# Held products at named places, a reordered first convolution and joins in small lots in a four-image, four-layer convolution kernel

## The chip, the cores and the metric

The kernel runs on one core of one Trainium2 chip. The metric is the device time of one execution in microseconds (us), as a median of three runs.

## The reference

Four layers work on x of shape (4, 256, 64, 64), all in fp32. Each adds to x what it computes from a group-normalised x (`_gn`: 32 groups, so 8 channels each):

```
x = x + L0(_gn(x))   # 3x3 convolution 256->256, group norm, relu = xs; then attention over 4096
                     #   pixels: softmax(theta^T phi) g, 128 wide; 1x1 to 256, group norm,
                     #   times 0.1, plus xs
x = x + L1(_gn(x))   # channel norm; q, k, v of 4 heads x 32; softmax of q over the head's channels,
                     #   of k over pixels; context = k v^T; out = context q; 1x1 to 256; channel norm
x = x + L2(_gn(x))   # two small nets (1x1, relu, mean) generate a depthwise 3x3 kernel for each
                     #   channel and a 256x256 pointwise matrix for each image; apply both, plus bias
x = x + L3(_gn(x))   # a router (mean, 64, softmax over 4 experts) mixes four 256x256 matrices;
                     #   apply the mixture
```

## The kernel before, in words

One image is held as two halves of 128 channels (h, or oh for outputs) by 4096 pixels. The four images go through a pipeline written out by hand: every engine's instructions run in the order in which the program emits them (`manual_schedule`). TensorE is given the order by interleaving two generators: `attend(b)`, 256 steps of logits (`pf`), exponentials (`pr`, ScalarE), row sums (`tot`, VectorE) and weighted values (`py`), and a `Chain`, which carries the layers after the attention of the image before (`tail`: `nonlocal_out`, `linear_attention`, `generated`, `mixed`) and then the convolution of the next image (`convolve`). A chain's parts yield costs; each time their sum times the chain's rate passes 1, one attention step is emitted and `tick` runs the functions that were put off with `later(n, f)`. The rate is 1.5 beside image 0's attention, 0.86 beside those of images 1 and 2, 1.24 beside that of image 3.

**Convolution.** The 3x3 convolution is done with transformed filters: six filter rows a (0 to 5) and, inside a row, four products k in the order 1, 2, 0, 3. `down` makes the rows of an input by VectorE, `across` the operand `v` of a product, `products` runs eight matmuls into two PSUM banks (`ps_conv`, L399), `joined` adds them, and `joining` adds a whole filter row into the four output rows y0 to y3: for a = 2 three operations for each half, for a = 4 six. In `convolve` these joins of row 2 are put off by one tick, both halves together; those of row 4 go into a list, `rest`, and leave it three per tick through `some`. `convolve_first` does image 0, where no attention runs beside it: rows 0, 1, 2 and 5 are taken as plain matmuls over shifted rows (`row_products`, `ps_row`, L431), rows 3 and 4 as products; filters for the later images are made by `filter_across` and stored to DRAM (12 DMAs each on SP). Then come statistics (`stats`, L389), the group norm (`group_finish`: aggregate L295, two small matmuls `pm` L300 and `pv` L309 with VectorE steps between and after them, and a root on POOL, L206) and `normed_relu`.

**End phase.** The last layer of image 2 (`mixed`) does not run beside image 3's attention: its 16 products (`product`: four matmul instructions `ps_ex`, L1086, into one bank; then a sum `res` on VectorE, L117, and a store on SP) are put into a list `held`. The last chain, `end`, runs image 3's tail after its attention and takes them out. `w.room` says how many may go; each tick takes one while there is room, and its sum is emitted one tick later.

In that tail, `linear_attention` normalises 512 pixels at a time (`normed`, ScalarE), sums squares (`norms`: `ps_ss`, L752, and a root on POOL), multiplies (`qkv`: `ps_qkv`, L765), and accumulates the context; a small chain (`cm`, `ps_cm`, `ps_w2`) follows, then eight rounds of `outputs` (`ps_o`, L830, four squares on ScalarE, root on POOL), `scaled` and `added` (transposes `ps_zt`, L853). `generated` computes the hidden layer (`ps_h`, L903), normalises into xp, gets the tap factors dk and sets nine diagonal matrices `diag` (ScalarE, L996). Its eight parts (c, h) of 1024 pixels are split for the last image: five (`mine`) are done by VectorE, `centre` on ScalarE (L941) and eight taps (L117, 1.3 us each), three (`others`) by TensorE with the diagonals (`ps_dw`, L984), nine for each 512 pixels, let out by a credit per tap. `pointwise` (`ps_pw`, L949) and its sums follow each pair of parts. `mixed` computes the router and `wm` and runs image 3's own 16 products.

Of the kernel before, what the change touches and what calls it, by code (L numbers as in the profile page):

```python
# [10 lines left out]
ALU = mybir.AluOpType  # L11
# [3 lines left out]
NH = 2  # L15
HW = 64
# [27 lines left out]
class Chain:  # L44
# [3 lines left out]
    def __init__(self, layers, rate=1.0, held=()):  # L48
        self.layers, self.rate, self.due = layers(self), rate, []
        self.held, self.room = held, 0  # L50

    def fill(self):

        if self.room > 0 and self.held:
            self.room -= 1
            self.later(1, self.held.pop(0)())
# [9 lines left out]
    def tick(self):  # L66

        due = [(k - 1, f) for k, f in self.due]
        self.due = [d for d in due if d[0] > 0]
        for k, f in due:  # L70
            if k <= 0:
                f()
        self.fill()
# [13 lines left out]
def conv_preact_fast(ctx: ExitStack, tc: tile.TileContext, guard, x, wc, wtpg, ww, wqkv, wout, w1cat, wd2,  # L87
# [199 lines left out]
    def stats_tile():  # L287
        return sp.tile([P, NH, 8, 6], F32, name="st")
# [203 lines left out]
    def convolve(w, b):  # L492
# [19 lines left out]
        def join(a, k, ps):  # L512
            dst = joined(a, k, ps)
            if k == 3 and a == 4:

                for oh in range(NH):
                    rest.extend(joining(a, oh, dst[oh]))
                for j in range(4):
                    w.later(1 + j, lambda: some(3))
                for j in range(3):  # L520
                    w.later(5 + j, lambda j=j: stats(j))
            elif k == 3:
                some(len(rest))
                for oh in range(NH):
                    w.later(1, lambda oh=oh: rows_joined(a, oh, dst[oh]))
# [25 lines left out]
    def convolve_first(w):  # L551
# [27 lines left out]
        two = row_products(2, ra)  # L579
# [5 lines left out]
        for oh in range(NH):  # L585
            rows_joined(2, oh, two[oh])
        for i, (a, k, v, f) in enumerate(four):
            if i + 1 < TX:
                joined(*three[i + 1])
            four[i] = (a, k, products(a, k, v, f))  # L590
        y3 = row_products(5, rb)
        for a in (0, 1, 2, 5):
            filter_across(a)
        for i in range(1, TX):
            t = joined(*four[i])
        for oh in range(NH):
            rows_joined(4, oh, t[oh])
# [96 lines left out]
    def nonlocal_out(w, b, big, k4, xs_in):  # L694
# [18 lines left out]
        w.room += 2  # L713
# [3 lines left out]
        st = stats_tile()  # L717
        for i, (c, h) in enumerate(PARTS):
            cols = bass.ts(c, CH)
            wy, xs = parts[i]  # L720
            stt(big[:, h, cols], wy, sc[:, h:h + 1], xs, ALU.mult, ALU.add)
            if i + ahead < len(PARTS):
                parts.append(load_parts(i + ahead))
            yield 0.6
            for s in range(2):
                nc.vector.bn_stats(st[:, h, 2 * c + s, :], big[:, h, bass.ts(2 * c + s, 512)])
            yield 0.6
        return st, sh


    def linear_attention(w, b, big, qT, k4, st, sh, alone):
        w.room += 2
# [25 lines left out]
        def qkv(xg, rinv):  # L758
# [3 lines left out]
            for j in range(4):  # L762
                ps = bank("ps_qkv")
                for h in range(NH):
                    nc.tensor.matmul(ps[:, 0:3 * HID], xg[:, h, bass.ts(j, P)], wqkv_s[:, h, :],  # L765
                                     start=(h == 0), stop=(h == NH - 1))
                nc.scalar.activation(qk[:, j, :], ps[:, 0:2 * HID], AF.Exp, scale=rinv[:, j:j + 1])  # L767
                nc.scalar.activation(v1[:, j, 0:P], ps[:, 2 * HID:3 * HID], AF.Copy, scale=rinv[:, j:j + 1])
                yield 0.125
# [20 lines left out]
        ready = ahead[0], norms(ahead[1])  # L790
        last = None
        for c in range(NC):
# [4 lines left out]
            if c + 1 < NC:  # L797
                ready = ahead[0], norms(ahead[1])
# [4 lines left out]
        w.room += 2  # L803
        context(NC - 1, *last)
        rk = sp.tile([P, 1], F32, name="rk")
# [13 lines left out]
        stt(w2, pw[:, 0:NH * P], HD * float(HD) ** -0.5, bo_s, ALU.mult, ALU.add)  # L819
        yield 1  # L820
# [37 lines left out]
        for c in range(NC):  # L858
# [4 lines left out]
            last = scaled(*zb)  # L863
            yield 0.6
        yield 1
        added(NC - 1, last)
        return st
# [4 lines left out]
    def generated(w, b, big, k4, st, sh, diag):  # L872
# [35 lines left out]
        for c in range(N // 512):  # L908
# [4 lines left out]
            if diag is not None and h == 1:  # L913
                nc.vector.tensor_scalar(*normed, rstd[:, h:h + 1], nb[:, h:h + 1], ALU.mult, ALU.add)
            else:
                nc.scalar.activation(*normed, AF.Identity, bias=nb[:, h:h + 1], scale=rstd[:, h:h + 1])
            yield 0.5
# [6 lines left out]
        nc.tensor.matmul(ppl[:, 0:2 * R], ones[0:HT * HP, :], pd, start=True, stop=True)  # L924
        pb = sp.tile([P, 2 * R], F32, name="pb")
# [67 lines left out]
        products, credit = taps_by_products(others), 0.0  # L993
        if diag is not None:
            for k in range(9):
                nc.scalar.activation(diag[:, k, :], ident, AF.Copy, scale=dk[:, 9 + k:10 + k])  # L996
        dw = {mine[0]: centre(mine[0])}
        slices = [load_wp2(0), load_wp2(1)]
        for n, i in enumerate(mine):
            if n + 1 < len(mine):  # L1000
                dw[mine[n + 1]] = centre(mine[n + 1])
            for wait in taps(i):

                credit += 18 * len(others) / (8 * (len(mine) - 1))
# [25 lines left out]
    def mixed(w, b, big, k4, st, sh, held):  # L1030
# [4 lines left out]
        w.room += 7  # L1035
# [23 lines left out]
        nc.vector.tensor_scalar(al, al, asum, None, ALU.mult)  # L1059
        wm = k2("wm")  # L1060
# [32 lines left out]

        for c in range(N // 512):
# [45 lines left out]
    with tc.manual_schedule(engines={E.PE, E.Activation, E.DVE, E.Pool, E.SP}):  # L1140
# [22 lines left out]
        for room, _ in zip((2, 0, 2, 1), attention):  # L1163
            end.room += room
            end.tick()
            if room == 2:
                end.fill()
        run(last)
        while held or end.due:
            end.room += 1  # L1170
            end.tick()
# [584 lines left out]
```

## Time and profile before

| | |
|---|---|
| median of 3 runs | 3176.08 us (3174.74 to 3176.4) |
| the profiled execution | 3175.36 us, span 3173.5 us |
| mean granted TensorE clock | 0.986 |
| busy share: TensorE, VectorE, ScalarE, POOL | 96%, 65%, 36%, 4% |
| first convolution, to the first `ps_tp` | 0 to 152.6 us |
| end phase, from the end of image 3's attention steps | about 2862 to 3173.5 us |

The page divides the span into 40 slices of 79.3 us; each digit is an engine's busy share in tenths. A timeline row holds the start, the duration, the engine, the line, the operation, its output and inputs with shapes, the count, and in brackets the idle time of the engine before it with what released it. fp32 matmuls of a 128x512 operand appear as two records each; four records are one held product.

### The profile page before, as it was taken

The numbers are of one execution on the slowest core, as the hardware profiler recorded it, in microseconds if no ns is written. First come the engines' busy times: TensorE is split into PE (matmuls) and PEld (weight loads), VectorE is DVE, ScalarE is ACT, GpSimd is POOL, SyncE is SP. The second block draws the span as 40 slices with busy tenths as digits, with TensorE's granted clock in tenths as the row PEclk, the third lists the DMA queues.
The fourth block names the chain that finished last, engine by engine and source line by source line (L and its number), as shares of the span: only waits on it lengthen the run. The fifth ranks groups of instructions, "written<-read, shape, count | busy, mean of one in ns | idle before, by whom it ended". The sixth has DMA issues, their size and how long they took to land.

```text
span 3173.5 us, 24226 instructions
## 1 busy us (share of the span) xinstructions
PE 3035.6 (96%) x8526; PEld 1472.2 (46%) x8526; DVE 2075.4 (65%) x2605; ACT 1132.1 (36%) x2099; POOL 129.6 (4%) x175
## 2 busy tenths in 40 slices
PE   6899999999999999999999999999999999996887
PEld 3354444445564444444565444444545544443533
DVE  8636676442547995777536896878363768855575
ACT  2133224333555332313364432312445453333520
POOL 0000000000010000000011000000100100000100
PEclk9999999999999999999999999999999999998999
DMA  5520113001100023113300102310410010121102
GB/s 182 169 45 24 33 35 65 7 14 47 67 11 27 14 73 119 37 37 67 113 10 1 40 20 83 105 41 30 110 64 1 11 34 13 47 73 47 45 6 74
DMA packets 73985, 161.68 MB, mean 51 GB/s; under 512 B 7936, under 2 KB 39424, under 8 KB 70912
## 3 DMA queue, kind: packets, MB, share of 16 engines
q1 hardware_dynamic: 69248, 143.27, 13.3%
q0 software_dynamic: 4608, 16.78, 2.9%
q8 instruction: 70, 1.15, 0.2%
q14 instruction: 59, 0.48, 0.0%
HBM read 103.40 MB, written 73.40 MB: 56 GB/s over the span
## 4 chain that ended last, share of the span: by engine, by line
PE 79%; DVE 13%; issue 5%; ACT 2%; DMA 0%; POOL 0%; SPq 0%; POOLq 0%; ACTq 0%
PE pf L637 23%; PE py L676 23%; PE ps_conv L399 8%; PE ps_qkv L765 5%; DVE dw L117 4%; PE ps_tp L613 4%; PE ps_ex L1086 3%; PE ps_pw L949 3%; DVE tot L114 2%; PE ps_g L618 2%; PE ps_wy L660 2%; PE ps_o L830 1%; PE ps_ctx L785 1%; PE ps_ss L752 1%; PE pss L649 1%
## 5 line engine op out<-in xcount | busy, mean ns | idle before, releaser
L638 ACT ACTIVATE pr<-pf 128x512 f32<-128x512 f32 x1024 | 604.4, 596 | 1229.2 <-PE pf L637 1216.0
L637 PE MATMUL pf<-tpg 128*128 128x512 f32 x2048 | 968.3, 595 | 1.4 <-ACT pr L638 1.4
L676 PE MATMUL py<-pr,tpg 128*128 128x512 f32 x2048 | 962.1, 592 | 3.0 <-ACT pr L638 2.9
L114 DVE TENSOR_TENSOR tot<-tot,pr 128x1024 f32<-128x1024 f32 x448 | 546.2, 1219 | 253.1 <-ACT pr L638 251.5
L676 PEld LDWEIGHTS py<-pr,tpg 128*128 128x128 f32 x2048 | 388.8, 190 | 494.5 <-issue 479.3
L637 PEld LDWEIGHTS pf<-tpg 128*128 128x128 f32 x2048 | 382.3, 190 | 444.4 <-issue 419.8
L117 DVE SCALAR_TENSOR_TENSOR dw<-xp,dk,dw 128x1008 f32<-128x1008 f32 x224 | 282.9, 1267 | 7.0 <-ACT dw L941 3.6
L399 PE MATMUL ps_conv<-v,u 128*128 128x512 f32 x576 | 261.7, 601 | 12.7 <-issue 9.0
L399 PEld LDWEIGHTS ps_conv<-v,u 128*128 128x128 f32 x576 | 110.8, 193 | 154.4 <-issue 147.3
L765 PE MATMUL ps_qkv<-wqkv_s,xg 128*128 128x384 f32 x384 | 130.3, 489 | 0.0
L613 PE MATMUL ps_tp<-big,wtpg_s 128*128 128x512 f32 x256 | 117.1, 601 | 3.0 <-ACT big L488 3.0
L114 DVE TENSOR_TENSOR tpg<-ps_g,bg_s 128x512 f32<-128x512 f32 x32 | 22.1, 691 | 144.7 <-PE ps_g L618 144.7
L206 POOL TENSOR_TENSOR rstd<-rstd,half 128x2 f32<-128x2 f32 x24 | 16.8, 700 | 2445.2 <-DVE rstd L311 2251.5
L949 PE MATMUL ps_pw<-dw,pk 128*128 128x512 f32 x224 | 103.8, 597 | 10.3 <-DVE dw L117 10.3
L651 DVE RECIPROCAL inv<-pss 128x512 f32<-128x512 f32 x32 | 107.3, 3352 | 7.2 <-PE pss L649 7.2
L773 DVE TENSOR_REDUCE qs<-qk 128x16 f32<-128x512 f32 x24 | 16.5, 686 | 123.4 <-ACT qk L767 123.4
L765 PEld LDWEIGHTS ps_qkv<-wqkv_s,xg 128*128 128x128 f32 x384 | 72.0, 190 | 52.4 <-issue 8.6
L114 DVE TENSOR_TENSOR v<-ra 128x1024 f32<-128x1024 f32 x72 | 86.7, 1219 | 0.4
L614 ACT ACTIVATE tpg<-ps_tp,btp_s 128x512 f32<-128x512 f32 x64 | 43.8, 687 | 118.7 <-PE ps_tp L613 118.5
L949 PEld LDWEIGHTS ps_pw<-dw,pk 128*128 128x128 f32 x224 | 42.7, 192 | 65.1 <-issue 51.2
L613 PEld LDWEIGHTS ps_tp<-big,wtpg_s 128*128 128x128 f32 x256 | 47.6, 193 | 54.5 <-issue 50.0
L832 ACT ACTIVATE junk<-ps_o 128x256 f32<-128x256 f32 x128 | 49.2, 384 | 63.6 <-PE ps_o L830 60.6
(278 smaller groups left out, 2887.1 us busy)
## 6 DMA issues: line engine op xcount, KB each, us to landing
u<-filters SPq DMA_DIRECT2D x144, 128.0 KB, 2.3
xp<-in_x_dram SPq DMA_DIRECT2D x16, 1024.0 KB, 6.2
xs_d<-big POOLq DMA_DIRECT2D x32, 512.0 KB, 11.6
wy_d<-wt SPq DMA_DIRECT2D x32, 512.0 KB, 3.0
out_dram<-res SPq DMA_DIRECT2D x64, 256.0 KB, 2.0
wy<-wy_d SPq DMA_DIRECT2D x28, 512.0 KB, 5.3
xs<-xs_d SPq DMA_DIRECT2D x24, 512.0 KB, 5.3
wp<-in_wp_dram SPq DMA_DIRECT2D x16, 512.0 KB, 4.6
```

The costliest lines, as they stand in the source:

```text
L114: nc.vector.tensor_tensor(o, a, b, op)
L117: nc.vector.scalar_tensor_tensor(o, a, s, b, op0, op1)
L399: nc.tensor.matmul(ps[oh], u(oh, h), v[:, bass.ts(h, 512)], start=(h == 0), stop=(h == NH - 1))
L613: nc.tensor.matmul(ps, wtpg_s[:, h, k, :], big[:, h, cols], start=(h == 0), stop=(h == NH - 1))
L618: nc.tensor.matmul(ps[:, j, :], big[:, h, bass.ts(4 * c + j, P)], wtpg_s[:, h, 2, :], start=(h == 0), stop=(h == NH - 1))
L637: nc.tensor.matmul(pf, phi[:, bass.ts(2 * m + s, P)], theta[:, bass.ts(q, 512)], start=True, stop=True)
L638: nc.scalar.activation(pr[:, bass.ts(s, 512)], pf, AF.Exp)
L651: nc.vector.reciprocal(inv, pss)
L676: nc.tensor.matmul(py, g[:, bass.ts(2 * m + s, P)], probs[i][:, bass.ts(s, 512)], start=(m == 0 and s == 0), stop=(m == NM - 1 and s == 1))
L765: nc.tensor.matmul(ps[:, 0:3 * HID], xg[:, h, bass.ts(j, P)], wqkv_s[:, h, :], start=(h == 0), stop=(h == NH - 1))
L949: nc.tensor.matmul(ps, pk[:, h * NH * P + oh * P:h * NH * P + (oh + 1) * P], dw[h][:, bass.ts(s, 512)], start=(h == 0), stop=(h == NH - 1))
L1086: nc.tensor.matmul(ps, wm[h][:, bass.ts(oh, P)], big[:, h, cols], start=(h == 0), stop=(h == NH - 1))
```

## The change

It has three parts.

1. *Held products.* `Chain` loses `room`. `fill(n)` emits n held products at once where it stands, and keeps their sums in `unsettled`; `settle()` emits these sums where it stands. Ticks take nothing any more. The 16 products now go: two beside the last softmax sums of the attention, two ahead of the eight sums of `nonlocal_out`, one ahead of `cm`, one after each of the output rounds c = 2 and 4, two after the last round, one after the hidden layer, three after `ps_pool`, three after the router's softmax.
2. *Image 3's tail and all linear attentions.* The first `ps_qkv` product of an image is emitted ahead of its norm sums. In `generated` with `diag`, the second half of h = 0 is normalised by VectorE rather than ScalarE; `centre` of the first part stands ahead of the diagonals; the credit per tap is 18 x 3 / (8 x 5) = 1.35 diagonal products rather than 18 x 3 / (8 x 4) = 1.69.
3. *Convolutions.* In `convolve` the six joins of row 2 go through `rest`, two per tick over three ticks. In `convolve_first` row 2 comes after the products of row 4, the filters of rows 0, 1, 2 and 5 are made inside the loop over row 4's products, and rows 2 and 4 are joined by a new sequence, seven operations for each half and then eight with row 2.

```diff
@@ -47,13 +47,18 @@
 
     def __init__(self, layers, rate=1.0, held=()):
         self.layers, self.rate, self.due = layers(self), rate, []
-        self.held, self.room = held, 0
-
-    def fill(self):
-
-        if self.room > 0 and self.held:
-            self.room -= 1
-            self.later(1, self.held.pop(0)())
+        self.held, self.unsettled = held, []
+
+    def fill(self, n):
+
+        for _ in range(min(n, len(self.held))):
+            self.unsettled.append(self.held.pop(0)())
+
+    def settle(self):
+
+        for f in self.unsettled:
+            f()
+        self.unsettled = []
 
     def later(self, n, f):
 
@@ -70,7 +75,6 @@
         for k, f in due:
             if k <= 0:
                 f()
-        self.fill()
 
     def steps(self):
         credit = 0.0
@@ -519,6 +523,11 @@
                     w.later(1 + j, lambda: some(3))
                 for j in range(3):
                     w.later(5 + j, lambda j=j: stats(j))
+            elif k == 3 and a == 2:
+                for oh in range(NH):
+                    rest.extend(joining(a, oh, dst[oh]))
+                for j in range(3):
+                    w.later(1 + j, lambda: some(2))
             elif k == 3:
                 some(len(rest))
                 for oh in range(NH):
@@ -576,25 +585,34 @@
         row_products(0, ra)
         go(down(2, ra, rb))
         row_products(1, rb)
-        two = row_products(2, ra)
         go(down(3, rc))
         three = [(a, k, products(a, k, v, u)) for a, k, v, u in across_all(3, rc)]
         go(down(4, rb, rc))
         four = across_all(4, rb)
         go(down(5, rb))
-        for oh in range(NH):
-            rows_joined(2, oh, two[oh])
         for i, (a, k, v, f) in enumerate(four):
             if i + 1 < TX:
                 joined(*three[i + 1])
+            filter_across((0, 1, 2, 5)[i])
             four[i] = (a, k, products(a, k, v, f))
+        two = row_products(2, ra)
         y3 = row_products(5, rb)
-        for a in (0, 1, 2, 5):
-            filter_across(a)
         for i in range(1, TX):
             t = joined(*four[i])
+
         for oh in range(NH):
-            rows_joined(4, oh, t[oh])
+            y0, y1, y2, y3_ = (image[:, oh, :, j, :] for j in range(MY))
+            both = k4("both").rearrange("p (y x) -> p y x", x=HW)
+            tt(both, y3_, t[oh], ALU.add)
+            tt(y3_, y3_, t[oh], ALU.subtract)
+            tt(y0, y0, both, ALU.add)
+            tt(y0, y0, y1, ALU.add)
+            stt(y2, both, 4.0, y1, ALU.mult, ALU.add)
+            stt(y1, y3_, 2.0, y1, ALU.mult, ALU.add)
+            stt(y3_, y3_, 6.0, y1, ALU.mult, ALU.add)
+        for j, op in enumerate((ALU.add, ALU.subtract, ALU.add, ALU.subtract)):
+            for oh in range(NH):
+                tt(image[:, oh, :, j, :], image[:, oh, :, j, :], two[oh], op)
         for j in range(3):
             stats(j)
         for y, ps in y3:
@@ -710,11 +728,11 @@
         parts = [load_parts(i) for i in range(ahead)]
         if xs_in is not None:
             yield 1
-        w.room += 2
         bias = vec_s[:, V_WB, :]
         _, gm, rstd = yield from group_finish(wy_stats[b], avg32, 1e-5, bias)
         sc, sh = affine(gm, rstd, vec_s[:, V_G2W, :], vec_s[:, V_G2B, :], bias, 0.1)
         st = stats_tile()
+        w.fill(2)
         for i, (c, h) in enumerate(PARTS):
             cols = bass.ts(c, CH)
             wy, xs = parts[i]
@@ -725,11 +743,11 @@
             for s in range(2):
                 nc.vector.bn_stats(st[:, h, 2 * c + s, :], big[:, h, bass.ts(2 * c + s, 512)])
             yield 0.6
+        w.settle()
         return st, sh
 
 
     def linear_attention(w, b, big, qT, k4, st, sh, alone):
-        w.room += 2
         _, gm, rstd = yield from group_finish(st, avg8, 1e-5, sh)
         nb = norm_bias(gm, rstd, sh)
         pctx = bank("ps_ctx")
@@ -755,7 +773,8 @@
             rsqrt(rinv, rinv)
             return rinv
 
-        def qkv(xg, rinv):
+        def qkv(xg, s2, rinv):
+
             qk = k4("qk").rearrange("p (j o) -> p j o", j=4)
             v1 = k4("v1")[:, 0:4 * (P + 1)].rearrange("p (j o) -> p j o", j=4)
             nc.gpsimd.memset(v1[:, :, P:P + 1], 1.0)
@@ -764,6 +783,8 @@
                 for h in range(NH):
                     nc.tensor.matmul(ps[:, 0:3 * HID], xg[:, h, bass.ts(j, P)], wqkv_s[:, h, :],
                                      start=(h == 0), stop=(h == NH - 1))
+                if rinv is None:
+                    rinv = norms(s2)
                 nc.scalar.activation(qk[:, j, :], ps[:, 0:2 * HID], AF.Exp, scale=rinv[:, j:j + 1])
                 nc.scalar.activation(v1[:, j, 0:P], ps[:, 2 * HID:3 * HID], AF.Copy, scale=rinv[:, j:j + 1])
                 yield 0.125
@@ -787,7 +808,7 @@
 
         ahead = normed(0)
         yield 1
-        ready = ahead[0], norms(ahead[1])
+        ready = *ahead, None
         last = None
         for c in range(NC):
             if c + 1 < NC:
@@ -795,13 +816,13 @@
             yield 0.5
             this = yield from qkv(*ready)
             if c + 1 < NC:
-                ready = ahead[0], norms(ahead[1])
+                ready = *ahead, norms(ahead[1])
             if last is not None:
                 context(c - 1, *last)
             last = this
         yield 1
-        w.room += 2
         context(NC - 1, *last)
+        w.fill(1)
         rk = sp.tile([P, 1], F32, name="rk")
         nc.vector.reciprocal(rk, pctx[:, P:P + 1])
         cm = k2("cm")[:, 0:P]
@@ -817,6 +838,7 @@
         nc.tensor.matmul(pw[:, 0:NH * P], cmT, wout_s, start=True, stop=True)
         w2 = k2("w2")[:, 0:NH * P]
         stt(w2, pw[:, 0:NH * P], HD * float(HD) ** -0.5, bo_s, ALU.mult, ALU.add)
+        w.settle()
         yield 1
 
         st = stats_tile()
@@ -861,9 +883,13 @@
             if last is not None:
                 added(c - 1, last)
             last = scaled(*zb)
+            w.settle()
+            if c in (2, 4):
+                w.fill(1)
             yield 0.6
         yield 1
         added(NC - 1, last)
+        w.fill(2)
         return st
 
 
@@ -910,10 +936,13 @@
                 hidden(c)
             h, q = c % 2, c // 2
             normed = xin[:, h, bass.ts(q, CH // HW), :], big[:, h, bass.ts(q, CH)].rearrange("p (y x) -> p y x", x=HW)
-            if diag is not None and h == 1:
+            if diag is not None and (h == 1 or q > 1):
                 nc.vector.tensor_scalar(*normed, rstd[:, h:h + 1], nb[:, h:h + 1], ALU.mult, ALU.add)
             else:
                 nc.scalar.activation(*normed, AF.Identity, bias=nb[:, h:h + 1], scale=rstd[:, h:h + 1])
+            if c == NC3:
+                w.settle()
+                w.fill(1)
             yield 0.5
         pooled = sp.tile([HT * HP, 1], F32, name="pooled")
         nc.vector.tensor_reduce(pooled, hs, AX.X, ALU.add)
@@ -922,6 +951,7 @@
         yield 1
         ppl = bank("ps_pool")
         nc.tensor.matmul(ppl[:, 0:2 * R], ones[0:HT * HP, :], pd, start=True, stop=True)
+        w.fill(3)
         pb = sp.tile([P, 2 * R], F32, name="pb")
         nc.vector.tensor_copy(pb, ppl[:, 0:2 * R])
         dkp = k2("dkp")[:, 0:NH * 9 * R].rearrange("p (k r) -> p k r", r=R)
@@ -991,17 +1021,18 @@
         mine = [i for i, (c, h) in enumerate(PARTS) if diag is None or h == 0 or c == 0]
         others = [i for i in range(len(PARTS)) if i not in mine]
         products, credit = taps_by_products(others), 0.0
+        dw = {mine[0]: centre(mine[0])}
+        w.settle()
         if diag is not None:
             for k in range(9):
                 nc.scalar.activation(diag[:, k, :], ident, AF.Copy, scale=dk[:, 9 + k:10 + k])
-        dw = {mine[0]: centre(mine[0])}
         slices = [load_wp2(0), load_wp2(1)]
         for n, i in enumerate(mine):
             if n + 1 < len(mine):
                 dw[mine[n + 1]] = centre(mine[n + 1])
             for wait in taps(i):
 
-                credit += 18 * len(others) / (8 * (len(mine) - 1))
+                credit += 18 * len(others) / (8 * len(mine))
                 while credit >= 1:
                     credit -= 1
                     next(products, None)
@@ -1032,7 +1063,6 @@
         for j in range(NE // 2):
             ex.append(pool4("ex").rearrange("p (k o) -> p k o", k=2))
             nc.sync.dma_start(out=ex[j], in_=experts[:, bass.ts(j, 2), :])
-        w.room += 7
         mv, gm, rstd = yield from group_finish(st, avg8, 1e-5, sh)
         off = sp.tile([P, NH], F32, name="off")
         tt(off, gm, sh, ALU.subtract)
@@ -1057,6 +1087,7 @@
         nc.scalar.activation(al, pl[:, 0:NE], AF.Exp, bias=nm, accum_out=asum)
         nc.vector.reciprocal(asum, asum)
         nc.vector.tensor_scalar(al, al, asum, None, ALU.mult)
+        w.fill(3)
         wm = k2("wm")
         for j in range(NE):
             if j == 0:
@@ -1091,6 +1122,7 @@
                 return lambda: nc.sync.dma_start(out=out[b, bass.ts(oh, P), cols], in_=res)
             return added
 
+        w.settle()
         for c in range(N // 512):
             for oh in range(NH):
                 if held is not None:
@@ -1160,15 +1192,13 @@
         while next(attention, False):
             pass
         next(last)
-        for room, _ in zip((2, 0, 2, 1), attention):
-            end.room += room
-            end.tick()
-            if room == 2:
-                end.fill()
+        for part, _ in enumerate(attention):
+            if part == 0:
+                end.fill(2)
+            elif part == 2:
+                end.settle()
         run(last)
-        while held or end.due:
-            end.room += 1
-            end.tick()
+        assert not held and not end.unsettled
 @with_exitstack
 def conv_preact_general(ctx: ExitStack, tc: tile.TileContext, x, wc, wtpg, ww, wqkv, wout, w1cat, wd2,
                        bd2, wp2, bp2, experts, rw1, rw2, vec, btp, bg, bo, b1cat, out):
```

## The prediction

> **What bounds the kernel now.** I read the slices first, then idle TensorE time by windows of 20 us, then the timelines of the places that the change touches. Slices:
>
> ```profile
> PE   6899999999999999999999999999999999996887
> DVE  8636676442547995777536896878363768855575
> ```
>
> TensorE is full from slice 3 to slice 35; the rest is the first convolution and the end phase of the last image (from 2862 us), where VectorE and chains of small dependent steps decide. Inside the full part the windows show few holes; the two longest are alike, in the convolutions of images 2 and 3. Image 2 in the timeline:
>
> ```profile
> 1365.76 2.48 DVE L114 TENSOR_TENSOR big<-big,t 128x1024 f32<-128x1024 f32 x2
> 1368.15 1.22 DVE L114 TENSOR_TENSOR big<-big 128x1024 f32<-128x1024 f32 x1
> 1369.29 2.48 DVE L114 TENSOR_TENSOR big<-big,t 128x1024 f32<-128x1024 f32 x2
> 1371.68 1.22 DVE L114 TENSOR_TENSOR big<-big 128x1024 f32<-128x1024 f32 x1
> 1372.82 1.22 DVE L117 SCALAR_TENSOR_TENSOR ra<-rt,ra 128x1024 f32<-128x1024 f32 x1
> 1374.07 1.23 DVE L114 TENSOR_TENSOR v<-ra 128x1024 f32<-128x1024 f32 x1
> 1375.39 5.18 PE L399 MATMUL ps_conv<-v,u 128*128 128x512 f32 x8 [4.52 <-issue]
> ```
>
> Six joining operations of filter row 2 stand together ahead of the `v` that the next product needs: TensorE idles 4.52 us, then the same eight matmuls take 5.18 us instead of the 3.60 seen elsewhere. The first convolution ends on VectorE:
>
> ```profile
> 134.72 7.21 DVE L389 BATCH_NORM_STATS2 st<-big 128x6 f32<-128x512 f32 x12
> 141.86 2.46 DVE L114 TENSOR_TENSOR big<-big,ps_row 128x512 f32<-128x512 f32 x4
> 144.24 2.46 DVE L389 BATCH_NORM_STATS2 st<-big 128x6 f32<-128x512 f32 x4
> 146.62 0.58 DVE L295 BATCH_NORM_AGGREGATE mv<-st 128x2 f32<-128x48 f32 x2
> 147.54 0.56 PE L300 MATMUL pm<-mv,avg 128*128 128x2 f32 x2 [9.58 <-DVE mv L114]
> ```
>
> The 9.58 says that TensorE had finished at 137.96. In the end phase, held products of image 2 stand ahead of small steps:
>
> ```profile
> 2870.57 0.75 DVE L117 SCALAR_TENSOR_TENSOR res<-ps_ex,b,big 128x512 f32<-128x512 f32 x1 [0.41 <-PE ps_ex L1086]
> 2872.29 0.75 DVE L117 SCALAR_TENSOR_TENSOR res<-ps_ex,b,big 128x512 f32<-128x512 f32 x1 [0.97 <-PE ps_ex L1086]
> 2872.96 0.59 DVE L295 BATCH_NORM_AGGREGATE mv<-wy_st 128x2 f32<-128x48 f32 x2
> ...
> 2900.05 3.76 PE L1086 MATMUL ps_ex<-big,wmh 128*128 128x512 f32 x4
> 2903.61 0.42 PE L309 MATMUL pv<-ev,avg 128*128 128x2 f32 x2
> ...
> 3081.90 0.69 DVE L114 TENSOR_TENSOR tpg<-ps_pw,tpg 128x512 f32<-128x512 f32 x1 [2.11 <-PE ps_pw L949]
> ...
> 3112.37 2.07 PE L949 MATMUL ps_pw<-dw,pk 128*128 128x512 f32 x2 [8.30 <-DVE dw L117]
> ```
>
> Sums wait for TensorE ahead of the aggregate; `pv` waits behind a product; VectorE waits for a product queued behind diagonal ones; later TensorE idles 8.30 us.
>
> **What the Trainium skill says.** "TensorE: Matmul & The Clock Gate", Part 1: The HAM clock gate: after about 3.4 us idle the clock is halved, after about 3.4 us of sustained work it is full again, in free-running windows. The trace agrees roughly: a held product (four matmuls) takes 1.72 us warm and 3.62 at 2900, and full speed returned 3 to 6 us after work began. The same page, Part 2, "Step-by-step": matmuls stay in program order, only weight loads are pulled ahead; it agrees, as `pv` above shows. Its "Architectural detail" section: VectorE and ScalarE are strict FIFO; the joins above agree. "PSUM — Partial Sum Buffer", Specifications: eight banks of 512 fp32; the kernel's pool has eight, and no wait in this trace shows their limit.
>
> **The change, part by part.**
>
> *Convolutions of images 1 to 3.* The six joins go out two per tick over three ticks. Two instead of six stay ahead of `v`: 4 x 1.19 (7.12/6) = 4.7 us earlier against a wait of 4.52. The slow matmuls that followed (5.18 and, in image 3, 6.53 against 3.60) go too: 6.1 and 7.4 us. In image 1 the rate of 1.5 brings all three ticks before `v`; its 2.03 us wait stays. The other four joins land behind `v`, where VectorE idles 2.0 us (image 2) and 3.3 us (image 3) soon after; if that is too little the next product waits. Sum -13.5, bounds -15.5 (image 1 gains too) and -6.
>
> *First convolution.* `row_products(2)` moves behind the products of row 4, the four `filter_across` into their loop, rows 2 and 4 are joined together: 22 joins of 1.22 instead of 18 (+4.9 us of VectorE). TensorE's order becomes rows 0, 1, 3, 4, 2, 5 with the same matmuls, ending again at 137.96 if no bank is late: the eight products of row 3 fill all eight banks, and row 4 needs them at 86.5, 89.9, 93.4; walking VectorE's list (2.5 or 1.3 us joins, then 2.0 us filters, from 80.1) frees them at 82.6, 85.9 and 90.3. One `filter_across` waits for ScalarE, whose half-filter stands behind a `one` copy; about 1 us, in slack. The 14 joins of row 4 end near 116.5, the eight with row 2 wait for its last bank (118.2) and end at 126.9, twelve stats at 134.1. After 137.96 remain one sum (0.7) and four stats (2.46): aggregate at 141.2 instead of 146.6. The 48 filter DMAs (about 0.5 us each on SP) run from 84 to about 108 instead of 109 to 127; the next load on SP follows earlier and passes nothing. Sum -5.4, bounds -6.5 and 0.
>
> *First q, k, v product ahead of the norm sums.* In images 0 and 1 TensorE waits 1.1 us at the first `ps_ss`; the product covers it: -2.2. ScalarE's first exponential then waits for the root on POOL (1.0 us) no later than now (836.2 against 836.8). Bounds 0 and -5 (half clock near 836 gone too; ScalarE's queue delaying `pr`). In the last image: start at 2906.83 (inputs ready) instead of 2908.68, and the sums' 1.86 us hide less idle time; the warm clock also comes earlier. -2.2.
>
> *Held products, in order of time.*
> - Two behind `ps_wy` go: aggregate right after the stats (2870.2 for 2872.96), `pv` not behind a product (0.8): -3.6.
> - Two filled before the eight sums run while TensorE idles 22 us. Their sums stand before the next aggregate (2 x 0.7), one inside the loop goes (0.65): +0.7.
> - `pv` at 2901.03 for 2903.61: -2.6.
> - One stays beside `cm`; the second, ahead of `ps_w2` (2975.20, ready at 2974.0), goes: -1.2.
> - Outputs, after c = 2 and 4: a product (1.72) in a gap of about 1.3 us ahead of `ps_o`, with its start-up: +0.5 each, +1.0. Their sums (0.75) meet 0.6 us of VectorE idle.
> - Two after the last transposes: TensorE idles 2.9 us and the clock is half; 3.7 us for half of the eight matmuls and 1.6 for the rest put `pm` 2.4 us later, but `ps_h` (7.27 us, mostly at half clock) then runs in about 5: 0, bounds -0.5 and +3.
> - One after `ps_h`, three after `ps_pool` (5.2 us to about 3034). Half of head 0's normalising moves to VectorE (0.75 each, idle there) and `centre` ahead of the nine diagonals: taps could start 3.8 us earlier, but four sums stand before them and the last waits for its product: start at 3035.2 for 3034.99, +0.2. SP's second order: the wp2 loads, issued at 2977.84 now, queue behind these six stores; 2 MB from about 3036 at the 330 GB/s of that earlier burst lands by 3043, under the eight taps (to 3045.4). If the cover fails, 2 to 5 us.
> - Pacing: 1.35 instead of 1.69 diagonal products per tap. A product is 0.85 us, a part's 10.8 are 9.1 us, with 6.9 of pointwise 16.0, beside 15.8 of VectorE (before: 11.4 + 6.9). The VectorE waits 2.11 + 0.3 and 1.21 + 0.3 go, and the 8.30 us hole fills, so the last pointwise runs warm (-1.7 with the sums behind it). Against it: TensorE reaches the first pointwise some 8 us early, goes cold, and costs about 2 us there. -3.2, bounds -5 and 0.
> - Last block: `pv` 0.85, `ps_hid` 0.6, `ps_log` 1.3 and two sums among `wm` (1.5) go, 4.2 us. Three products after the softmax run cold, 7.4 us beside 4 of VectorE: 2.8 given back. The final loop then starts warm (29.02 us now, 27.5 at 0.43): -3.0, bounds -5 and 0.
>
> End phase with its own norm sums (-2.2): -13.9. All: -13.5 - 5.4 - 2.2 - 13.9 = **-35.0**. The profiled execution took 3175.36 us (span 3173.5), 0.7 below the median of 3176.08, so 3140.4 there and **3141** for a median. The bounds add to about -52 and -4; they won't all fall on one side, and I allow about -45 to -18.
>
> **Rivals.**
> - *Joins only displaced.* The four late joins delay the following `v`, and TensorE waits there instead. For: those windows show VectorE 96% busy. Against: it idles right afterwards. Without the 13.5: 3155. Chance 0.15.
> - *End phase gives nothing.* Cold products and sums ahead of the taps eat what the removed waits free. For: the half clock at each of these places. Against: the five removed waits are single and visible. 3155. Chance 0.2.
> - *Both*: 3168; with the first convolution also stalled on banks, 3174, no change. Chance 0.08 together.
> - *Slower: held work heads TensorE's queue at half clock.* Fourteen of the sixteen products now stand in the end phase's chain. If each ran cold (3.44 us) ahead of a step that something waits for, 48 us come on, against 35 less: 3189. It decides once about ten of them are on the chain. The 22 us hole and the finished `ps_h` speak against that. Chance 0.03.
> - *It doesn't do what it says*: in image 1 the pacing of joins already does nothing; that is in the sum.
>
> My forecast gets 0.54. A measurement of this kernel tells about 0.2% (6.4 us) from no change. Faster by more: 0.92; within: 0.05; slower: 0.03. The range 3130 to 3159 takes in the two single rivals.
>
> **What would show it.** The L399 waits of 4.52 us gone; the aggregate near 141; TensorE's hole before `pm` near 3 us; `pv` behind no product; four `res` before the taps; no 8 us hole ahead of the last pointwise, perhaps one ahead of the first. New L399 or `pr` waits inside the convolutions, or a chain that ends on `ps_ex` of held products at several places, would prove me wrong.

## The result and the profile after

The changed kernel takes **3145.15 us** (median of 4 runs, 3144.3 to 3146.26) against 3176.24 for the kernel before on the same chip: ratio 0.9903, 95% interval 0.9886 to 0.992. It is faster by 31.1 us; the forecast was 3141 with a range of 3130 to 3159. The profiled execution took 3145.76 us, with a span of 3144.0 against 3173.5: 29.5 us to explain.

The slices of the page hardly move; the change is in single places, so it has to be followed there. A *half-clock window* below is a stretch of 3.41 us, or of several times that, in which the trace has TensorE at half of its clock.

```profile
PE   6899999999999999999999999999999999996888
DVE  8736766443547995877536896778363768855485
```

In the timeline of image 2's convolution two joins (one row, x2) stand ahead of `v`, not six, and the product that waited 4.52 us starts with no idle time in brackets and at full speed (six matmuls in 2.81):

```profile
1358.73 2.48 DVE L118 TENSOR_TENSOR big<-big,t 128x1024 f32<-128x1024 f32 x2
...
1362.38 1.23 DVE L118 TENSOR_TENSOR v<-ra 128x1024 f32<-128x1024 f32 x1
...
1363.70 2.81 PE L403 MATMUL ps_conv<-v,u 128*128 128x512 f32 x6
```

The end of the first convolution: VectorE has caught up and now waits 3.03 us for TensorE's last rows. One sum and four stats remain, and TensorE's hole ahead of `pm` is 3.95 us where it was 9.58.

```profile
137.31 0.69 DVE L118 TENSOR_TENSOR big<-big,ps_row 128x512 f32<-128x512 f32 x1 [3.03 <-PE ps_row L435]
137.91 2.46 DVE L393 BATCH_NORM_STATS2 st<-big 128x6 f32<-128x512 f32 x4
140.30 0.58 DVE L299 BATCH_NORM_AGGREGATE mv<-st 128x2 f32<-128x48 f32 x2
...
141.22 0.35 PE L304 MATMUL pm<-mv,avg 128*128 128x2 f32 x2 [3.95 <-DVE mv L118]
```

In the end phase `pv` (2876.03) stands behind no product. Two output rounds hold one (2957.48, 2968.85), and their first square on ScalarE then waits 2.64 and 2.50 us. The 8.30 us of idle time ahead of the last pointwise product are gone; ahead of the first one there are 8.14, and that one is now cold, which here means that it runs in a half-clock window. `ps_b` waits behind three cold products although `wm` is ready at 3105.66:

```profile
2876.03 0.59 PE L313 MATMUL pv<-ev,avg 128*128 128x2 f32 x2 [0.84 <-DVE ev L118]
...
2957.48 3.57 PE L1117 MATMUL ps_ex<-big,wmh 128*128 128x512 f32 x4
...
2962.01 0.38 ACT L854 ACTIVATE junk<-ps_o 128x256 f32<-128x256 f32 x1 [2.64 <-issue]
...
2968.85 3.05 PE L1117 MATMUL ps_ex<-big,wmh 128*128 128x512 f32 x4
...
2972.84 0.38 ACT L854 ACTIVATE junk<-ps_o 128x256 f32<-128x256 f32 x1 [2.50 <-issue]
...
3036.82 2.07 PE L979 MATMUL ps_pw<-dw,pk 128*128 128x512 f32 x2 [8.14 <-DVE dw L121]
...
3042.34 0.69 DVE L118 TENSOR_TENSOR tpg<-ps_pw,tpg 128x512 f32<-128x512 f32 x1 [1.75 <-PE ps_pw L979]
...
3101.02 7.03 PE L1117 MATMUL ps_ex<-big,wmh 128*128 128x512 f32 x12
...
3107.89 0.95 PE L1108 MATMUL ps_b<-off,wm 128*128 128x1 f32 x8
```

Laid side by side, the two timelines account for the 29.5 us as follows (each row is the difference in length of a stretch between two instructions that both kernels have; the end phase runs from image 3's last `pss`).

| stretch | before, us | after, us | change | predicted |
|---|---|---|---|---|
| start to the first softmax | | | -5.6 | -5.4 |
| convolution of image 1 | | | +1.6 | 0 |
| convolutions of images 2, 3 | | | -6.2, -7.5 | -6.1, -7.4 |
| norm sums, images 0 and 1 | | | -3.0, -1.3 | -2.2 together |
| last `pss` to the aggregate of `nonlocal_out`'s norm | 11.32 | 8.44 | -2.9 | -2.8 (of the -3.6) |
| to the next aggregate | 25.75 | 25.69 | -0.1 | -0.8 (the rest) + 0.7 |
| to `ps_cm` | 74.66 | 70.34 | -4.3 | -4.8 |
| to `ps_o` | 2.94 | 1.84 | -1.1 | -1.2 |
| **output rounds**, to the aggregate | 38.86 | 44.22 | **+5.4** | **+1.0** |
| to `ps_pool` | 13.39 | 13.41 | 0 | 0 |
| taps, to the last aggregate | 94.08 | 91.78 | -2.3 | -3.0 |
| to the final loop, and its length | 14.18, 30.57 | 13.34, 29.13 | -2.3 | -3.0 |

The rounds before the change, for comparison: TensorE idles about 1.0 us ahead of the last six transposes of a round, and `ps_o` follows these without a break; from one `ps_o` to the next is 4.05 us.

```profile
2991.17 0.87 PE L853 MATMUL ps_zt<-ident,ra 128*128 128x128 f32 x6 [1.06 <-DVE ra L114]
2991.88 1.89 PE L830 MATMUL ps_o<-w,tpg 128*128 128x256 f32 x8
...
2995.22 0.87 PE L853 MATMUL ps_zt<-ident,z 128*128 128x128 f32 x6 [1.00 <-DVE z L114]
2995.93 1.89 PE L830 MATMUL ps_o<-w,tpg 128*128 128x256 f32 x8
```

### The profile page after: what moved, and what is told of

Same layout as the page of the kernel before. It is cut to its first block, busy times and chain, and to the rows that moved or that the text cites. A ratio compares the mean times of both kernels' runs of the same rounds, so it can differ in the third digit from the quotient of the medians.

```text
span 3144.0 us, 24213 instructions
## 1 busy us (share of the span) xinstructions
PE 3033.0 (96%) x8526; PEld 1472.9 (47%) x8526; DVE 2079.6 (66%) x2611; ACT 1129.2 (36%) x2097; POOL 131.6 (4%) x175
## 4 chain that ended last, share of the span: by engine, by line
PE 80%; DVE 12%; issue 5%; ACT 2%; DMA 0%; POOL 0%; SPq 0%; POOLq 0%; ACTq 0%
PE pf L655 23%; PE py L694 23%; PE ps_conv L403 8%; PE ps_qkv L784 5%; DVE dw L121 4%; PE ps_tp L631 4%; PE ps_ex L1117 3%; PE ps_pw L979 3%; DVE tot L118 2%; PE ps_g L636 2%; PE ps_wy L678 2%; PE ps_o L852 1%; PE ps_ctx L806 1%; PE ps_dw L1014 1%; PE ps_ss L770 1%
## 5 line engine op out<-in xcount | busy, mean ns | idle before, releaser
L121 DVE SCALAR_TENSOR_TENSOR dw<-xp,dk,dw 128x1008 f32<-128x1008 f32 x216 | 272.9, 1267 | 6.8 <-ACT dw L971 3.7
```

The source lines that it names most:

```text
L121: nc.vector.scalar_tensor_tensor(o, a, s, b, op0, op1)
```

## The experiments

Eleven kernels ran, in groups of four, four and three, each group on another chip with the kernel before beside it (medians 3176.54, 3175.77 and 3175.80 us). Differences below are to the changed kernel's 3145.15 (of medians) and to its trace (of stretches). The runs of one kernel spread over 1.6 to 3.9 us, so a difference of medians under about 1 us says nothing; stretches of a trace are finer.

**Theories.** A: each edit acts at its own place, by the wait that it removes or makes, and the places add; what failed is the price of the output rounds. Rival B: the gains are half-clock windows that fell elsewhere, and undoing an edit brings back little or something else.

### Three undoings and one move

u1: without the new branch, the joins of row 2 go out together again.

```diff
-            elif k == 3 and a == 2:
-                for oh in range(NH):
-                    rest.extend(joining(a, oh, dst[oh]))
-                for j in range(3):
-                    w.later(1 + j, lambda: some(2))
```

> The changed kernel with one part undone: in the convolutions of images 1 to 3 the six joins of filter row 2 stand together again. Theory (the joins were what made TensorE wait, and the slow matmuls behind it came from that wait): the waits of about 4.5 us before the products of ps_conv in images 2 and 3 are back, with slow matmuls behind them, about +13.7 us (6.2 + 7.5); image 1 either stays as it is or loses the 1.6 us it lost with the change, so about 3157 to 3159 us. Rival (the joins are only displaced, the stalls come from where the half-clock windows happen to fall): under +7 us, 3145 to 3152.

3154.81 us (3153.34 to 3155.69), +9.7: between the two. The trace says why:

```profile
1366.81 6.52 PE L403 MATMUL ps_conv<-v,u 128*128 128x512 f32 x8 [4.53 <-issue]
...
2968.58 1.88 PE L1112 MATMUL ps_ex<-big,wmh 128*128 128x512 f32 x4
```

The first line is the old wait with its slow matmuls; images 2 and 3 are 7.5 and 7.1 us longer, somewhat more than theory A wanted. But the end phase, whose code is untouched, became 5.2 us shorter: the second line is the product of the first output round at full clock, 1.88 us where the changed kernel has 3.57. The clock in the trace fits: this end phase has 51.2 us of half-clock windows, the changed kernel's 61.4, which is three windows fewer. Image 1 was 1.6 us shorter.

u2: the first convolution as before (that part of the diff reversed).

> The changed kernel with the first convolution as before. Theory (VectorE's tail after TensorE's last product is what was cut): the hole of TensorE ahead of pm is about 9.6 us again instead of 3.95, the first softmax 5.6 us later, and nothing else moves: about 3151 us (+5.6). Rival (later stages absorb the shift, since the end is set by other waits): under +2 us.

3149.48 us (3147.86 to 3151.13), +4.3. The start is 6.2 us longer, and no later stretch absorbs it. The profiled executions differ by 5.4 us in all, since image 1 is 1.7 us shorter here too, with the same joins as in the changed kernel. First the changed kernel, then u2, the same wait and the same eight matmuls:

```profile
389.83 5.40 PE L403 MATMUL ps_conv<-v,u 128*128 128x512 f32 x8 [1.90 <-DVE v L118]
```

```profile
396.04 3.70 PE L403 MATMUL ps_conv<-v,u 128*128 128x512 f32 x8 [1.91 <-DVE v L118]
```

So the +1.6 of image 1 is not the joins. The slow product is in the profiled execution of the changed kernel and of four of the eleven, and not in the other seven.

u3: norm sums ahead of the first q, k, v product in every image.

```diff
-                if rinv is None:
-                    rinv = norms(s2)
...
-        ready = *ahead, None
+        ready = *ahead, norms(ahead[1])
```

> The changed kernel with the norm sums of q and k ahead of the first q, k, v product again, in all images. Theory: the first ps_ss waits about 1.1 us again in images 0 and 1, together +4.3 us if a half-clock window near 836 us comes back as well, +2.2 without it; the last image +1.9 us. Together +4 to +6 us, 3149 to 3151. Rival (the gains in images 0 and 1 were only half-clock windows that fell elsewhere): about +1.9 us from the last image alone, 3147.

3151.82 us (3150.6 to 3152.24), +6.7, above theory A's range. Images 0 and 1 are 3.0 us longer each and the last image's way to `ps_cm` 1.8. Image 0 shows the two pieces, the wait and, 3 us later, a `pf` at half clock (3.06 for 1.88):

```profile
828.72 1.05 PE L770 MATMUL ps_ss<-ones,s 128*128 128x1 f32 x8 [1.11 <-DVE s L118]
...
831.52 3.06 PE L655 MATMUL pf<-tpg 128*128 128x512 f32 x4
```

u4: no products in the output rounds.

```diff
-            w.settle()
-            if c in (2, 4):
-                w.fill(1)
...
         st = stats_tile()
-        w.fill(2)
+        w.fill(4)
```

> The changed kernel with the two held products of the output rounds c = 2 and 4 moved ahead of the rounds: four instead of two are issued after the last transposes. Theory (a product among the rounds makes its round 2.7 us longer, as the changed kernel's timeline shows): rounds 5.4 us shorter; the two products ahead, beside TensorE's idle time there, cost 0 to 3.4 us in half-clock time. Together -2 to -5 us, 3140 to 3143. Rival (as the prediction had it, a product in a round costs 0.5 us and the rest of the 5.4 us has another cause): -1 us plus what the moved products cost, 3144 to 3147.

The expectation has four products issued after the last transposes; the edit, as shown, puts the two moved ones ahead of the eight sums of `nonlocal_out`. 3141.28 us (3140.39 to 3142.65), -3.9. The rounds take 38.84 us, as before the change (38.86), so the products in the rounds, with the clock that came with them, are the whole +5.4. Their new place costs 1.3 us (two more sums ahead of the aggregate) and about 1.0 up to `ps_cm`.

### Pace, hole and place

e5: the credit per tap as before.

```diff
-                credit += 18 * len(others) / (8 * len(mine))
+                credit += 18 * len(others) / (8 * (len(mine) - 1))
```

> The changed kernel with 1.69 instead of 1.35 diagonal products per tap again, all else as changed. Theory (as the prediction had it: the slower pace takes waits of VectorE for queued pointwise products away): +2 to +3 us, 3147 to 3148. Rival (the pace shifts TensorE's hole from the last pointwise product to the first, and gives nothing): within 1 us of 3145.

3152.81 us (3152.42 to 3155.07), +7.7: the pace is worth more than either theory said. The taps' stretch is 5.3 us longer, and VectorE's waits say where: the last pointwise product is cold behind its hole again, and the sum behind it waits 3.88 us (2.08 in the changed kernel); two earlier waits are 2.88 and 1.21 (0.34 each there). That is 5.2 us. The first pointwise product is cold in both, with the same wait of 1.75 us behind it, though the hole ahead of it is 3.05 us at the old pace and 8.14 at the new one. From its last sum to the end of the span that trace also has 8.9 us, the changed kernel's 6.8.

```profile
3089.37 2.08 PE L979 MATMUL ps_pw<-dw,pk 128*128 128x512 f32 x2 [8.29 <-DVE dw L121]
...
3093.19 0.69 DVE L118 TENSOR_TENSOR tpg<-ps_pw,tpg 128x512 f32<-128x512 f32 x1 [3.88 <-PE ps_pw L979]
```

e6: the three products behind `ps_pool` go into the hole (the comments in this cut and in the last one are for the reader).

```diff
-        w.fill(3)                      # behind ps_pool
...
             if n == 0:
                 ...                    # pk
+                w.fill(3)
+            if n == 1:
+                w.settle()
```

> The changed kernel with the three held products behind ps_pool issued later: behind the diagonal products of the first part, so that they stand in TensorE's 8 us hole ahead of the first pointwise product; their sums come ahead of that product instead of ahead of the taps. Theory (sums ahead of the taps wait for TensorE, 1.9 us, and the hole makes the first pointwise product cold, 1.75 us): -3 to -4.5 us, 3141 to 3142. Rival (VectorE is busy throughout this stage, and its three sums cost the same wherever they stand): -1 us to 0, 3144 to 3145.

3141.40 us (3139.94 to 3142.49), -3.75. The stretch of the taps is 4.6 us shorter. Products, sums and the first pointwise product in a row; the product has no idle time ahead of it and its two matmuls take 1.02:

```profile
3016.20 5.31 PE L1119 MATMUL ps_ex<-big,wmh 128*128 128x512 f32 x12
...
3031.28 2.06 DVE L121 SCALAR_TENSOR_TENSOR res<-ps_ex,b,big 128x512 f32<-128x512 f32 x3
3031.54 1.02 PE L978 MATMUL ps_pw<-ra,pk 128*128 128x512 f32 x2
```

The sums stayed as long as they were; most of what went is VectorE's waiting for them ahead of the taps (0.96 + 0.97) and the cold start (1.75). The first tap comes 2.6 us after `ps_pool`, against 6.2.

e7: the products of the rounds one place later.

```diff
             zb = outputs(c)
+            if c in (3, 5):
+                w.fill(1)
...
-            if c in (2, 4):
-                w.fill(1)
```

> The changed kernel with the two held products of the output rounds issued one place later: behind ps_o of rounds 3 and 5, ahead of the transposes ps_zt, not ahead of ps_o. Theory (ahead of ps_o the product delays ScalarE's squares, on which the round hangs; there is idle time of 1.0 us ahead of ps_zt): about +0.8 us a round instead of the +2.7 of the changed kernel's trace, together -3 to -4 us, 3141 to 3142. Rival (a product anywhere in a round brings a half-clock window, and that is most of the cost): within 1 us of 3145.

3142.18 us (3140.63 to 3142.76), -3.0. The rounds take 40.80 us, 2.0 more than without products, and nearly all of that is in one round:

```profile
2956.66 3.47 PE L852 MATMUL ps_o<-w,tpg 128*128 128x256 f32 x8
...
2959.92 2.03 PE L1117 MATMUL ps_ex<-big,wmh 128*128 128x512 f32 x4
...
2962.67 1.89 PE L852 MATMUL ps_o<-w,tpg 128*128 128x256 f32 x8
2966.65 1.89 PE L852 MATMUL ps_o<-w,tpg 128*128 128x256 f32 x8
2968.38 1.88 PE L1117 MATMUL ps_ex<-big,wmh 128*128 128x512 f32 x4
2970.97 1.89 PE L852 MATMUL ps_o<-w,tpg 128*128 128x256 f32 x8
```

From one `ps_o` to the next is 6.01 us with the first product and 4.32 with the second; without a product it is 4.04 to 4.11 in u4. The first round fell into a half-clock window (`ps_o` 3.47 for 1.89) that began before any product had run there, the second did not. So this place costs 0.2 us at full clock. The place ahead of `ps_o` costs 1.0 at full clock: in u1 the five rounds with both products, up to a later half-clock window, take 23.62 us (2963.25 to 2986.87), the same ones in u4 21.64.

e8: the kernel before with the two convolution parts alone.

> The kernel before with the two convolution changes alone (first convolution, and the joins of images 1 to 3). Theory (the parts add): 3176.5 - 5.6 - 13.7 = about 3157 us; what is left to the changed kernel, 12 us, is the norm sums (4 to 6) and the end phase (6 to 8). Rival (an end phase that is shifted against the half-clock windows changes by itself): more than 4 us away from 3157.

3161.24 us (3158.43 to 3162.28), 4.2 above the sum, just on the rival's side. The convolutions gave what they should in the trace (-5.0, -6.2, -7.5); against that stand image 1's slow product (+1.6), one more half-clock window at image 1's norm sums (+1.7) and an end phase 1.3 us longer than before with the very same code. Only the profiled run can be split so; its span is 14.0 below the one before. The first wait of the end phase and the way from `ps_cm` to `ps_o` are as long here as before (11.32 and 2.94), so what the changed kernel gains there does not come from the convolutions.

### Versions that follow

If the places add, the sixteen products can be dealt out anew: none in the rounds, more ahead of the eight sums (with their own sums put off behind the first norms, where VectorE idles 5.3 us), some in the hole, fewer behind the softmax.

```diff
-        w.fill(2)             # nonlocal_out
+        w.fill(5)             # b1: 5, b2: 4, b3: 5; its settle goes behind the first norms(s2)
...
+                w.fill(3)     # the hole, as in e6; b1: 3, b2: 4, b3: 4
...
-        w.fill(3)             # softmax
+        w.fill(2)             # b1: 2, b2: 2, b3: 1
```

> The changed kernel with its held products redistributed: five instead of two ahead of the eight sums of nonlocal_out, with their sums behind the first norms of linear_attention instead of ahead of the aggregate; none in the output rounds; the three of ps_pool in the hole ahead of the first pointwise product, as in e6_hole; two instead of three behind the softmax. Theory (each place has its own price, and they add): -1.3 us (two sums ahead of the aggregate gone), -5.4 (rounds), -4.4 (hole), -1.0 to -1.7 (one cold product less ahead of ps_b): 3132 to 3133 us. Rival (the half-clock windows move with the work and take part of it back, as in u1, which ended 5 us better than its joins cost): 3136 to 3139.

> As b1_five_three_two, but four ahead of the sums of nonlocal_out and four in the hole ahead of the first pointwise product. Theory (in e6_hole the first pointwise product started just when its operand was ready, so a fourth product there, 1.7 us, delays it): 0.5 to 1.7 us slower than b1. Rival (the hole of 8.1 us holds four, 6.9): equal to b1 within 0.5.

> As b1_five_three_two, but four products in the hole and one behind the softmax. Theory for the last block (ps_b waits for cold products, not for wm, which is ready 4.5 us after the softmax; one product, 3.4 us cold, ends before wm is ready): ps_b 1.0 to 1.9 us earlier than with two; with the fourth product in the hole at 0.5 to 1.7 us it is within 1 us of b1. Rival (with TensorE idle before ps_b the final loop starts at half clock, 1.7 us): 1 to 2.5 us slower than b1.

b1: 3133.55 us (3131.43 to 3134.79). b2: 3132.95 (3132.59 to 3135.0). b3: **3131.96** (3131.09 to 3133.4), ratio to the kernel before 0.9864 (0.9847 to 0.988), 13.2 us below the changed kernel. The medians of the three are too close to rank, and b1's is half a microsecond above theory A's range. The stretches of b1 are those of theory A: -1.3 to the second aggregate, -5.4 in the rounds, -4.6 in the taps, -1.4 to the final loop, +0.7 to `ps_cm`. A fourth product in the hole costs 0.7 (taps 87.83 for 87.17), at the lower end. With one product behind the softmax `ps_b` waits for `wm` and no longer for TensorE:

```profile
3088.59 3.75 PE L1117 MATMUL ps_ex<-big,wmh 128*128 128x512 f32 x4
...
3092.63 0.62 DVE L1103 TENSOR_SCALAR wm<-wm,rstd 128x256 f32<-128x256 f32 x2
3093.04 1.09 PE L1108 MATMUL ps_b<-off,wm 128*128 128x1 f32 x8 [0.70 <-DVE wm L1103]
```

From the last aggregate to the final loop is 10.94 us in b3, 11.93 in b1 and 13.34 in the changed kernel, and the loop takes 29.14 us in all of them, so the rival's slow loop did not come.

## Why the prediction was right, and where it was not

**Right by place.** Convolutions of images 2 and 3, the first convolution, the first wait of the end phase, `ps_cm` and `ps_w2`, and the nil ahead of `ps_pool` are within 0.5 us of their terms. The nil was two parts, as forecast: `pm` comes 2.2 us later behind cold products (2.4 forecast), and `ps_h` then takes 5.3 us instead of 7.3. u1, u2 and u3 show for the convolutions and the norm sums that the gains belong to these edits. The gains at the first wait, at `pv` and at `ps_w2` are read from the traces; no run undid them one by one, though in e8, without these edits, the first wait and `ps_w2` stayed as before. The two single rivals are out: "joins only displaced" by u1 (14.6 us in images 2 and 3 when undone), "end phase gives nothing" by the 7.6 us that the trace shows there.

**Wrong: the output rounds.** The term was 0.5 us for each product, "in a gap of about 1.3 us ahead of `ps_o`"; the stretch grew by 5.4 us for two. Two things were missed. First, the gap is not there: before the change TensorE's 1.0 us of idle time stands ahead of the last transposes, and `ps_o` follows these without a break. A product there pushes `ps_o` back, and with it ScalarE's squares, on which the round hangs; at full clock it costs 1.0 us each (u1 against u4), and behind `ps_o` only 0.2 (e7). Second, the clock was at risk in these rounds. The other 1.7 us each (5.4 less 2 x 1.0, halved) are half-clock windows: in the changed kernel one of 3.4 us lies on each of the two products. u3 fits the same prices: one window on a product, one on a round without a product (0.8 us, as in e8), and rounds 4.5 us longer than in u4 (2.0 + 1.7 + 0.8). The prediction reckoned with half clock at the last transposes, the first pointwise product and the softmax, and not here.

**Too large: the pace** (-3.2; from the first tap to the last aggregate the trace has -2.1). The last pointwise product's sum waits 2.08 us for 3.78, the 1.7 forecast, and the cold first one costs 1.75 + 0.25, the 2 forecast. But the waits of 2.11 and 1.21 shrink to 0.34 each, and the 0.30 behind each stays: 2.6 us, where the term had 3.9 (its pieces add to -3.6, not -3.2). The start of the taps, +0.2 forecast, came 0.2 us earlier; without the three sums behind `ps_pool` it comes 3.6 us earlier still (e6), close to the 3.8 that the prediction names there. The prediction charged the cold first product to the slower pace, but e5 has it at the old pace too, behind a hole of 3.05 us, while in the kernel before a hole of 2.04 us left it warm; what made it cold is open. So undoing the pace alone costs 5.3 us: it brings the waits back and does not make the first product warm.

**Too large: the last block** (-3.0; the trace -2.3). Two of its terms held: the loop that starts warm (-1.4 for -1.5) and what the cold products give back beside the two sums saved (+1.2 for 2.8 - 1.5). The mis-sized term is the waits of `pv`, `ps_hid` and `ps_log` behind products: 2.0 us went by `ps_log`, where the sum had 2.75. And b3 shows what the give-back was: two of the three products, 2.4 us.

**Too small: the norm sums.** -2.2 for images 0 and 1 counted only the 1.1 us wait; the trace has -3.0 and -1.3, and u3 brings back 3.0 us in each, the wait with a half-clock window behind it. With the norm sums first, that window came in both images of u3 and of e8, but in the kernel before only in image 0. The prediction had this as a bound (-5).

**Image 1's +1.6** is no part of the change: the same code ran without it in u2 and u3.

The sum was 35.0, and 29.5 came in the trace. The rounds alone are 4.4 of the 5.5 us that are missing and image 1 is 1.6; the other errors nearly cancel, the norm sums' against those of the pace and the last block, and that is luck.

**Open.** What sets a half-clock window is not settled. In the changed kernel TensorE is busy for 1.42 and 1.84 us of the 3.41 us ahead of the two windows in the rounds, and in u1's rounds those with 2.04 us or more were followed by full clock. But the busy share alone does not decide: in image 1's convolution a stretch of 3.41 us with 1.51 us of work (from 387.29) was followed by half clock in the changed kernel, and one with 1.50 (from 392.69), in the same code, by full clock in u2. Nor is the shortening of u1's end phase by 5.2 us explained further than that three windows fewer fell into it.

## What to carry to other kernels

A hole of an engine in a chain of small dependent rounds is not free room: ask what starts on the instruction behind the hole, and put filler behind the one that the round hangs on (0.2 us here) rather than ahead of it (1.0). Put a product where its engine has a long hole and its consumer idles later, and let the two places differ (`fill` and `settle`): the same sixteen products gave 13 us more when dealt out by measured prices. When a hole is closed, look at where idle time appears instead and what is cold behind it: the new pace closed the 8 us hole ahead of the last pointwise product and lengthened the one ahead of the first from 3 to 8 us. That first product was cold at either pace, and it was products put into its hole that took this cost away.

## What had not been expected of the hardware

The half clock came in rounds of 4 us, and ahead of the two windows TensorE was never idle for more than 1.1 us at a time. The Trainium skill ("TensorE: Matmul & The Clock Gate", Part 1: The HAM clock gate) has the cold state come after at least one idle window of about 3.4 us. These runs differ: stretches of 3.41 us with 1.42 and 1.84 us of work were followed by half clock in the changed kernel, and of two with 1.5 us of work in the same code one was followed by half clock, the other (in u2) by full. Such a window costs what it uncovers: 0.8 us on the rounds of e8, which hold no product, about 1.7 on a round with one.

Whole stretches of identical code differ by what stands ahead of them: the end phase took 305.8 us before the change and 307.1 in e8, and the one of the changed kernel lost 5.2 us when only joins, the last of them some 700 us earlier, were undone. A change of a few microseconds in such a kernel has to be read from the stretch where it acts, not from the total.
